# Turning 24 row tiles of a fused two-matmul kernel by DMA instead of on TensorE

## The chip, the cores and the metric

The kernel runs on one core of a Trainium2 chip. The metric is the device time of one execution, in microseconds (us): the time before is the median of three runs. TensorE (PE) multiplies and can also turn (transpose) a 128x128 block; VectorE (DVE) and ScalarE (ACT) do the element-wise work; GpSimd (POOL) and SyncE (SP) issue transfers here. Sixteen DMA engines move the data of the core.

## The reference

The two inputs are `x` (2 batches x 1024 rows x 2048) and a context (2 x 2048 x 2048); a weight of 2048 x 2048 is shared by both batches. Cut to what matters:

```python
# fake_quant: round to integers 0..255 about a zero point of 128, and back
# first product: rows normalised, quantised, times the quantised context of their batch
q1 = fake_quant(layernorm(x), x1_scale, x1_zp)
q2 = fake_quant(ctx_4096, x2_scale, x2_zp)
x = x + tanh(g_xattn) * matmul(q1, q2)
# second product: rows normalised again, quantised to -128..127 by each row's maximum,
# times a weight that is rounded to -1, 0 or 1
n = layernorm(x)
s = 127 / max(abs(n), axis=-1)
q = clip(round(n * s), -128, 127) / s
tw = clip(round(weight / mean(abs(weight))), -1, 1)
x = x + tanh(g_ffn) * einsum('bsi,oi->bso', q, tw) * mean(abs(weight))
```

## The kernel before

**Tiles.** The rows are 16 row tiles of 128 rows: 0 to 7 are batch 1, 8 to 15 batch 2. Eight row tiles of `x` (`resid`) are resident; a tile of batch 2 takes the place of the tile of batch 1 with the same number less 8, once that tile's result is stored. Everything else of size lives in the `arena`, 32 slots of 4 KB in each of 128 partitions (`NS`): loads of context and weight take two neighbouring slots, a quantised context unit takes one, a turned row tile takes one, and the eight quantised weight blocks one each. A second pool, `bytes_`, holds quantised rows as signed bytes (`NB`, 4 buffers of 128x2048, the pool `q8`). In PSUM there are three tiles `mm` of 128x1024 f32 for products and two tiles `tr` for turns.

**Steps.** For each batch: `norm1` takes the mean and variance of a pair of row tiles on DVE (L531, L536), a root on ACT (L540), scale and bias on DVE (L476 to L550), and the cast to bytes on ACT (L567). `first` (L622) multiplies a turned row tile by eight context units for one half of the columns (h is 0 or 1; 32 matmuls in eight steps), and DVE adds the result to `resid` (L628). Context units are loaded (L589), cast on ACT (L593) and clipped on DVE (L597). `norm2` does the second norm for a pair: a square on ACT (L660), its maximum on DVE (L666), a chain of small operations, and the cast to bytes on ACT (L716). The second product uses f16 rows and the ternary weight in fp8. In batch 1 it is `couple` (tiles 0 to 3, L759) and `plain` (tiles 4 to 7, L805); in batch 2 it is `seven` (L930), which computes each pair of row tiles with seven block products in place of eight, from sums of row halves (L895 to L902) and from sums and differences of weight blocks. Those are formed on DVE in `differences` (L842), written to DRAM (L861) and fetched back later (L871). DVE adds the second product to `resid` (L743), and SP stores it (L750). The weight is read twice: first for its mean (L977, L990, L992), then to be quantised (L1028), turned (L1035) and clipped (L1043, L1045).

**Turning a row tile.** `turn_steps` is the function that the change is about. A quantised row tile is 128 rows of 2048 bytes. Seen as 1024 two-byte values it is eight blocks of 128x128, and PE turns each block, a pair of bytes as one value, into a `tr` tile (L494). The pairs are then opened: two copies of 128x1024 bytes each, on ACT or DVE, whichever ends sooner, read the bytes from PSUM with a stride of two and write them as f16 into the tile's arena slot (L502). The byte buffer is free once PE has read it. All 32 turns go this way (16 tiles, two norms), and so do the 16 weight rows.

**The order.** No engine's order is written by hand. Each step is recorded with its engine (or a choice of engines), a weight in us, a due time, the keys that it reads and writes, and the buffers that it takes and gives back. `Order.run` plays the steps against a model: each engine does one step at a time, a transfer occupies one common DMA server for `dma` us and lands `LANDING` (2.0 us) later, and of the steps that could start first the one with the earliest due time is picked. `work_back` goes through the result backwards and gives every step a new due time. `give_out` repeats this 12 times and emits the instructions in the order of the best play, so that the order on every queue, SP's and POOL's among them, is fixed before the kernel runs. An engine works through its own list strictly in that order and waits where an operand is late. Some steps also have a hold, a time in the model before which they don't start: loads of batch 2, and `differences` at 210.

Of the kernel before, what the change touches and what calls it, by code (L numbers as in the profile page):

```python
# [11 lines left out]
I16 = mybir.dt.int16  # L12
F8 = mybir.dt.float8e4
AF = mybir.ActivationFunctionType
ALU = mybir.AluOpType
# [8 lines left out]
class Plan:  # L24
# [9 lines left out]
    def step(self, engine, weight, due, do, rd=(), wr=(), take=None, give=(), dma=0.0, hold=0.0):  # L34
        n = len(self.steps)
        after = set()
        for key in rd:
            if key in self.writer:
                after.add(self.writer[key])
        for key in wr:  # L40
            after.update(self.readers.pop(key, ()))
            if key in self.writer:
                after.add(self.writer[key])
            self.writer[key] = n
        for key in rd:
            self.readers.setdefault(key, []).append(n)
        after.discard(n)
        self.steps.append((engine, weight, due, do, after, take, tuple(give), dma, hold))
        return n
# [58 lines left out]
class Order:  # L108
# [64 lines left out]
    def run(self, due):  # L173
        steps, N = self.steps, len(self.steps)
        waits = [len(s[3]) for s in steps]
        early = [s[7] for s in steps]
        pools = {k: [(0.0, -1)] * n for k, n in self.sizes.items()}
        left = dict(self.users)
        till = {}
        free, open_ = {}, {}  # L180
        dma_free, dma_last = 0.0, -1
        begin, end, where, slots = [0.0] * N, [0.0] * N, [None] * N, [None] * N
        pred = [[] for _ in steps]
        links = self.links = [{} for _ in steps]
        last = {}
        order = []

        def put(n):
            for e, w in steps[n][0]:
                open_.setdefault(e, {})[n] = w  # L190

        for n in range(N):
            if not waits[n]:
                put(n)
        for _ in range(N):
            best = None
            for e, cand in open_.items():
                fe = free.get(e, self.START.get(e, self.BRANCH))
                for n, w in cand.items():
                    at = early[n]  # L200
                    if at < fe:
                        at = fe
                    if best is not None and at > best[0] + 1e-6:
                        continue
                    take = steps[n][4]
                    if take:
                        at = max(at, self.room(pools[take[0]], *take[1:]))
                        if at == float("inf"):
                            continue
                    if len(steps[n][0]) > 1:  # L210
                        key = (at, due[n], n, at + w, e)
                    else:
                        key = (at, due[n], n, 0.0, e)
                    if best is None or at < best[0] - 1e-6 or key[1:] < best[1:]:
                        best = key
            if best is None:
                self.stuck = [n for c in open_.values() for n in c], order, slots
                return None
            at, _, n, _, e = best
            ways, _, _, _, take, give, dma, _ = steps[n]  # L220
            if len(ways) > 1:
                ends = []
                for e2, w2 in ways:
                    ends.append((max(at, free.get(e2, self.BRANCH)) + w2, e2, w2))
                fin, e, w = min(ends)
                at = fin - w
            else:
                w = ways[0][1]
            for e2, _ in ways:
                del open_[e2][n]  # L230
            if take:
                pool = pools[take[0]]
                idx = slots[n] = self.pick(pool, at, *take[1:])
                for i in idx:
                    if pool[i][1] >= 0:
                        pred[n].append(pool[i][1])
                        links[n][pool[i][1]] = True
                    pool[i] = (float("inf"), -1)
            if e in last:
                pred[n].append(last[e])  # L240
            last[e] = n
            begin[n] = at
            where[n] = e
            fin = at + w
            free[e] = fin
            if dma:
                if dma_last >= 0:
                    pred[n].append(~dma_last)
                dma_free = max(dma_free, fin) + abs(dma)
                dma_last = n  # L250
                fin = dma_free + self.LANDING
            end[n] = fin
            order.append(n)
            for m, i in give:
                for j in range(steps[m][4][1]) if i is None else (i,):
                    left[m, j] -= 1
                    t = till.get((m, j))
                    if t is None or fin + self.LAG > t[0]:
                        t = (fin + self.LAG, n)
                    till[m, j] = t  # L260
                    if not left[m, j]:
                        pools[steps[m][4][0]][slots[m][j]] = t
            for m in self.follow[n]:
                same = len(steps[m][0]) == 1 and steps[m][0][0][0] == e and not dma
                t = fin + (0.0 if same else self.LAG)
                if t > early[m]:
                    early[m] = t
                waits[m] -= 1
                if not waits[m]:
                    put(m)  # L270
        return order, begin, end, where, slots, pred
# [72 lines left out]
def centred(  # L344
# [15 lines left out]
    nc = tc.nc  # L360
# [5 lines left out]
    MT, OT = M // P, O // P  # L366
# [1 line left out]
    H, U = 1024, 512  # L368
    NQ = N // U
    I8 = mybir.dt.int8  # L370
    NS, NB = 32, 4
    SLOT = 2048

    const = ctx.enter_context(tc.tile_pool(name="const", bufs=1))
# [28 lines left out]
    def slot16(s):  # L403
        return arena[:, s * SLOT : (s + 1) * SLOT]
# [30 lines left out]

    Q_COST = {"PRE": 0.5, "SP": 0.5, "POOL": 0.7}
    turned = {}

    def parameters():
        s = {}  # L440
# [32 lines left out]
    def rsqrt(v, sd):  # L473
# [7 lines left out]
        nc.vector.scalar_tensor_tensor(r, e, 1.5, r0, ALU.add, ALU.mult)  # L481
        return r

    def turn_steps(t, key, q, q_by, due, name, pieces=1):

        s = {}

        def turn(i, slots=None):
            if slots is not None:
                s["pt"] = tr[slots[0]]  # L490
            pt = s["pt"].bitcast(F16).rearrange("p (c r) -> p c r", c=C)
            v = q["q"].bitcast(F16)
            for c in range(i * C // pieces, (i + 1) * C // pieces):
                nc.tensor.transpose(pt[:, c, :], v[:, ts(c, P)], ident)  # L494

        def spread(h, engine, slots=None):
            if h == 0:
                turned[name, t] = slots[0]
            d = slot16(turned[name, t]).rearrange("p (c j m) -> p c j m", c=C, j=2)
            v = s["pt"].bitcast(I8).rearrange("p (c m j) -> p c j m", c=C, j=2)  # L500
            n = C // 2
            (nc.scalar.copy if engine == "ACT" else nc.vector.tensor_copy)(  # L502
                d[:, ts(h, n)], v[:, ts(h, n)]
            )

        by = None
        for i in range(pieces):
            n = step(
                "PE", 0.05 + 0.55 / pieces, due - 50, (lambda i: lambda slots=None: turn(i, slots))(i),
                rd=[key("q", i)], wr=[key("pt", i)], take=None if i else ("tr", 1),  # L510
                give=[q_by] if i == pieces - 1 else [],
            )
            by = by if i else n
        ways = (("ACT", 1.1), ("DVE", 1.3))
        first_ = step(
            ways, 0, due - 20, lambda e, slots: spread(0, e, slots), rd=[key("pt", 0)], wr=[(name, t, 0)],
            take=("ar", 1, 0, home_t), give=[by],
        )
        step(
            ways, 0, due - 20, lambda e: spread(1, e), rd=[key("pt", pieces - 1), (name, t, 0)],  # L520
            wr=[(name, t, 1)], give=[by],
        )
        turned[name, t, "by"] = first_
# [357 lines left out]
    def seven(ta, tb, due, final=False):  # L881
# [22 lines left out]
        qa, qb = ([("qT", t, i) for i in range(2)] for t in (ta, tb))  # L904
        by = step("DVE", 0.7, due - 3, lambda slots: sums(0, slots), rd=qb, wr=[("S", ta, 1)], take=("ar", 2, 0, pairs_d))
        step("DVE", 0.7, due - 3, lambda: sums(1), rd=qa[:1], wr=qb[:1] + [("S", ta, 3)])
        step("DVE", 0.7, due - 3, lambda: sums(2), rd=qa[:1] + [("S", ta, 1)], wr=[("S", ta, 2)])
        step("DVE", 0.7, due - 3, lambda: sums(3), rd=qa[1:] + [("S", ta, 2)], wr=[("S", ta, 4)])
        products = (
            ("P1", "A", lambda: half(ta, 0), (0, 0), qa[:1], True, (ta, 0)),  # L910
            ("P2", "C", lambda: half(ta, 1), (0, 1), qa[1:], True, (ta, 0)),
# [109 lines left out]
    def weight_turn(ot, due):  # L1021
# [15 lines left out]
        def clip(h, engine, slots=None):  # L1037
# [10 lines left out]
            "ACT", 2.1, due, quant, rd=[("wl", ot), ("sw",)], wr=[key("q")], take=("q8", 1),  # L1048
            give=[wl[ot]["by"]],
        )  # L1050
        p = step("PE", 0.6, due - 50, turn, rd=[key("q")], wr=[key("pt")], take=("tr", 1), give=[by])
        for h in range(2):
            need = [key("pt")] + ([("w", q, 0, h)] if o else [])
# [946 lines left out]
```

## Time and profile before

| What | Value |
|---|---|
| median of three runs | 492.32 us (491.85, 492.32, 495.02) |
| the profiled execution | 494.64 us, its span 492.9 us |
| busy: PE, DVE, ACT, POOL | 457.8, 335.1, 262.8, 21.7 us |
| PE's products: first (L622), second of batch 1 (L759, L805), second of batch 2 (L930) | 229.8; 58.5 and 55.9; 97.5 us |
| PE's turns: rows (L494), weight (L1035) | 256 and 128 instructions |
| copies out of the turns of rows (L502) | 39 on ACT, mean 1.01 us; 25 on DVE, mean 1.22 us |
| moved by DMA | 102.20 MB, mean 207 GB/s |

The span runs from the first to the last instruction of the profiled execution. Busy times are sums over an engine's instructions, without waits. A PE instruction is modelled as longer than its share of PE's time, since matmuls overlap: 1024 of L622 at a mean of 383 ns are busy for 229.8 us together. The granted TensorE clock was at full speed (0.998 in the mean). In time, the first product of batch 1 runs from about 39 to 156 us, the second of batch 1 from 131 to 271 us (the two are mixed between 131 and 156), the first of batch 2 from 271 to 388 us and the second of batch 2 from 388 to 487 us.

### The profile page before, as it was taken

What the parts mean: (1) busy time and instruction counts of PE and PEld (TensorE: products, weight loads), DVE (VectorE), ACT (ScalarE), POOL (GpSimd) and SP (SyncE); (2) the same over time, 40 slices, a digit from 0 to 9 for tenths busy, and PEclk for the clock granted to TensorE, in tenths of its full rate; (3) what the DMA queues carried; (4) which work ended last, traced back from release to release, by engine and by line L of the source; (5) the groups of instructions that cost most, each with busy time, mean ns of one, the idle gap of its engine ahead of it and who ended that gap; (6) DMA issues with size and microseconds to landing.
All of it is one profiled execution on the core that took longest, in us unless ns stands there. A gap on an engine that the chain in (4) does not pass through costs nothing.

```text
span 492.9 us, 6309 instructions
## 1 busy us (share of the span) xinstructions
PE 457.8 (93%) x2564; PEld 225.6 (46%) x2564; DVE 335.1 (68%) x522; ACT 262.8 (53%) x203; POOL 21.7 (4%) x39
## 2 busy tenths in 40 slices
PE   0489999999999898999998989999999999999995
PEld 0134444445576654444444435444444444444442
DVE  4778973588599897769997877223578887343432
ACT  3678987687799988831117678101366853000000
POOL 0000000000002120021011100000000000000000
PEclk9999999999999999999999999999999999999999
DMA  6999988990445985399999750053000012231304
GB/s 208 397 423 421 421 319 332 420 429 41 172 172 231 367 302 211 91 343 391 422 345 325 257 215 1 1 179 163 1 0 1 1 43 88 85 128 44 128 8 169
DMA packets 21853, 102.20 MB, mean 207 GB/s; under 512 B 1976, under 2 KB 1976, under 8 KB 16696
## 3 DMA queue, kind: packets, MB, share of 16 engines
q1 hardware_dynamic: 15008, 67.11, 34.2%
q0 software_dynamic: 6800, 34.61, 19.6%
q8 instruction: 22, 0.36, 0.3%
q14 instruction: 15, 0.12, 0.1%
q10 hardware_dynamic: 8, 0.00, 0.0%
HBM read 80.74 MB, written 20.97 MB: 206 GB/s over the span
## 4 chain that ended last, share of the span: by engine, by line
PE 65%; DMA 14%; issue 12%; DVE 3%; ACT 3%; SPq 1%; POOL 1%; POOLq 0%; ACTq 0%
PE mm L622 41%; PE mm L930 20%; DMA arena<-in_ctx_dram 14%; PE tr L494 2%; ACT arena L593 1%; ACT bytes L567 1%; PE mm L805 1%; SPq L1961 1%; DVE strip L666 1%; POOL arena L589 1%; DVE arena L1045 1%; DVE arena L502 0%; DVE resid L743 0%; PE mm L759 0%; POOL arena L977 0%
## 5 line engine op out<-in xcount | busy, mean ns | idle before, releaser
L622 PE MATMUL mm<-arena 128*128 128x512 f16 x1024 | 229.8, 383 | 7.9 <-DVE arena L597 4.6
L622 PEld LDWEIGHTS <-arena 128*128 128x128 f16 x1024 | 99.6, 99 | 125.0 <-issue 9.3
L743 DVE SCALAR_TENSOR_TENSOR resid<-mm,am,resid 128x1024 f32<-128x1024 f32 (+1 forms) x53 | 58.1, 1097 | 59.7 <-PE mm L930 47.9
L930 PE MATMUL mm<-arena 128*128 128x512 fp8e4 x448 | 97.5, 379 | 0.0
L593 ACT ACTIVATE arena<-arena,scal 128x2048 int16<-128x2048 f32 x32 | 63.3, 1999 | 47.3 <-DMA arena<-in_ctx_dram 36.4
L628 DVE SCALAR_TENSOR_TENSOR resid<-mm,scal,resid 128x1024 f32<-128x1024 f32 x32 | 40.9, 1278 | 49.4 <-PE mm L622 38.1
L930 PEld LDWEIGHTS <-arena 128*128 128x128 f16 x448 | 43.7, 98 | 51.9
L759 PE MATMUL mm<-arena 128*128 128x128 fp8e4 (+1 forms) x448 | 58.5, 288 | 1.7 <-DVE resid L743 1.7
L805 PE MATMUL mm<-arena 128*128 128x512 fp8e4 x256 | 55.9, 379 | 0.0
L660 ACT ACTIVATE arena<-resid,strip 128x2048 f32<-128x2048 f32 x16 | 32.0, 1998 | 39.5 <-DVE strip L654 35.4
L502 ACT CAST arena<-tr 128x1024 f16<-128x1024 int8 x39 | 37.8, 1011 | 16.9 <-PE tr L494 7.5
L759 PEld LDWEIGHTS <-arena 128*128 128x128 f16 x448 | 33.4, 98 | 24.1 <-issue 2.0
L666 DVE TENSOR_REDUCE strip<-arena 128x1 f32<-128x2048 f32 x16 | 36.5, 2280 | 5.1 <-ACT arena L660 5.1
L531 DVE BATCH_NORM_STATS2 stats<-resid 128x6 f32<-128x512 f32 x64 | 39.7, 675 | 0.0
L805 PEld LDWEIGHTS <-arena 128*128 128x128 f16 x256 | 24.9, 98 | 29.5
L567 ACT ACTIVATE bytes<-resid,strip 128x2048 int8<-128x2048 f32 (+1 forms) x17 | 33.0, 1987 | 7.7 <-DVE strip L550 5.9
L716 ACT ACTIVATE bytes<-resid,strip 128x2048 int8<-128x2048 f32 x16 | 32.7, 2087 | 6.7 <-DVE strip L689 6.7
L842 DVE TENSOR_TENSOR arena<-arena 128x2048 fp8e4<-128x2048 fp8e4 x16 | 36.0, 2281 | 0.0
L502 DVE CAST arena<-tr 128x1024 f16<-128x1024 int8 x25 | 30.3, 1218 | 7.1 <-PE tr L494 6.8
L1028 ACT ACTIVATE bytes<-arena,scal 128x2048 int8<-128x2048 f32 x16 | 31.3, 1999 | 0.8 <-DVE scal L1014 0.8
L1045 DVE TENSOR_SCALAR arena<-tr 128x1024 fp8e4<-128x1024 int8 x23 | 27.3, 1216 | 6.1 <-PE tr L1035 6.1
L494 PE MATMUL tr<-ident,bytes 128*128 128x128 f16 x256 | 20.6, 225 | 11.5 <-ACT bytes L567 9.2
(59 smaller groups left out, 184.5 us busy)
## 6 DMA issues: line engine op xcount, KB each, us to landing
arena<-in_ctx_dram SPq DMA_DIRECT2D x16, 1024.0 KB, 15.4
arena<-in_L_ffn_weight_dram SPq DMA_DIRECT2D x16, 1024.0 KB, 12.6
arena<-in_ctx_dram POOLq DMA_DIRECT2D x16, 1024.0 KB, 8.7
out_dram<-resid SPq DMA_DIRECT2D x31, 512.0 KB, 4.7
arena<-in_L_ffn_weight_dram POOLq DMA_DIRECT2D x9, 1024.0 KB, 6.6
resid<-in_x_dram POOLq DMA_DIRECT2D x8, 1024.0 KB, 11.6
resid<-in_x_dram SPq DMA_DIRECT2D x7, 1024.0 KB, 14.7
awayT<-arena SPq DMA_DIRECT2D x8, 512.0 KB, 7.5
```

The source lines that it names most:

```text
L502: (nc.scalar.copy if engine == "ACT" else nc.vector.tensor_copy)(d[:, ts(h, n)], v[:, ts(h, n)])
L531: nc.vector.bn_stats(stats6[:, t % 4, c, :], res(t)[:, ts(c, 512)])
L567: nc.scalar.activation(q["q"][:, ts(g, w)], res(t)[:, ts(g, w)], AF.Identity, bias=s["bi"][:, i : i + 1], scale=s["sc"][:, i : i + 1],)
L593: nc.scalar.activation(slot16(slots[0]).bitcast(I16), s["w"], AF.Identity, scale=rs2)
L622: nc.tensor.matmul(pm[t][:, ts(q, U)], a[:, c, j, :], o[:, j, ts(q, U)], start=(c + j == 0), stop=(c + j == C),)
L628: nc.vector.scalar_tensor_tensor(v, pm[t], g1, v, ALU.mult, ALU.add, accum_out=acc[:, i : i + 1])
L666: nc.vector.tensor_reduce(s["vm"][:, n + i : n + i + 1], s["dev", t], AX.X, ALU.max)
L743: lambda: nc.vector.scalar_tensor_tensor(v, ps(), am2[:, t : t + 1], v, ALU.mult, ALU.add),
L759: nc.tensor.matmul(ps[:, o0 * P : o1 * P], a[:, c, j, :], w[:, j, o0:o1], start=(c + j == 0), stop=(c + j == C),)
L805: nc.tensor.matmul(s["pm"][:, ts(i, U)], a[:, c, j, :], w[:, j, :], start=(c + j == 0), stop=(c + j == C),)
L842: nc.vector.tensor_tensor(slot8(s[k, n])[:, w], slot8(at(a))[:, w], slot8(at(b))[:, w], op, saturate=False)
L930: nc.tensor.matmul(s[bank][:, ts(n, U)], a[:, c, j, :], v[:, c, j], start=new and c + j == 0, stop=c + j == 4, skip_group_check=not new,)
```

## The change

For the row tiles of batch 2 in both norms, and for all tiles of batch 1 in the second norm (`by_dma`, 24 of the 32 turns), a new function `turn_far` takes the place of PE's turn. One DMA on SP's queue turns the row tile's bytes, as 128x1024 two-byte values in eight blocks, from `bytes_` into the upper half of the tile's own arena slot. Two copies then open the pairs within the slot: the first (on ACT or DVE) reads the first half of the bytes and writes the slot's lower half; the second (on ACT only) reads the rest and writes the upper half, where the bytes themselves lie. The slot is taken and the byte buffer held from the issue of the DMA; the buffer is given back when the DMA has landed. The model gets 1.1 us on SP for the issue, 1.4 us on the common DMA server, and a landing 2.8 + 2.0 us after the issue whatever else is queued. There are five byte buffers instead of four. In `seven`, the slot of the pair's first tile is given back only when the two sums that read it (L900, L902) are done as well. The tiles of batch 1 in the first norm and the weight rows are turned as before; the branch for weights in the diff is not taken, since `by_dma` holds no weight.

```diff
-                fin = dma_free + self.LANDING
+                fin = dma_free + self.LANDING if dma > 0 else fin - 2 * dma + self.LANDING
...
-    NS, NB = 32, 4
+    NS, NB = 32, 5
...
+    by_dma = {(k, t) for k, lo in (("aT", MT), ("qT", 0)) for t in range(lo, 2 * MT)}
...
+    def turn_far(t, key, q, q_by, due, name):
+        def turn(slots):
+            turned[name, t] = slots[0]
+            d = slot16(slots[0]).bitcast(I16)[:, H:].rearrange("p (c r) -> p c r", c=C)
+            nc.sync.dma_start_transpose(d, q["q"].bitcast(I16))
+
+        def spread(h, engine):
+            d = slot16(turned[name, t]).rearrange("p (c j m) -> p c j m", c=C, j=2)
+            v = slot16(turned[name, t])[:, H:].bitcast(I8).rearrange("p (c m j) -> p c j m", c=C, j=2)
+            n = C // 2
+            (nc.scalar.copy if engine == "ACT" else nc.vector.tensor_copy)(d[:, ts(h, n)], v[:, ts(h, n)])
+
+        n = turned[name, t, "by"] = step(
+            "SP", 1.1, due, turn, rd=[key("q", 0)], wr=[(name, t, 0), (name, t, 1)], take=("ar", 1, 0, home_t),
+            give=[q_by], dma=-1.4,
+        )
+        step((("ACT", 1.1), ("DVE", 0.75)), 0, due, lambda e: spread(0, e), wr=[(name, t, 0)])
+        step("ACT", 1.1, due, lambda: spread(1, "ACT"), rd=[(name, t, 0)], wr=[(name, t, 1)])
+
     def turn_steps(t, key, q, q_by, due, name, pieces=1):
+        if (name, t) in by_dma:
+            return turn_far(t, key, q, q_by, due, name)
...
-        step("DVE", 0.7, due - 3, lambda: sums(2), rd=qa[:1] + [("S", ta, 1)], wr=[("S", ta, 2)])
-        step("DVE", 0.7, due - 3, lambda: sums(3), rd=qa[1:] + [("S", ta, 2)], wr=[("S", ta, 4)])
+        step("DVE", 0.7, due - 3, lambda: sums(2), rd=qa[:1] + [("S", ta, 1)], wr=[("S", ta, 2)], give=[turned["qT", ta, "by"]])
+        step("DVE", 0.7, due - 3, lambda: sums(3), rd=qa[1:] + [("S", ta, 2)], wr=[("S", ta, 4)], give=[turned["qT", ta, "by"]])
```

## The prediction

> **What bounds the kernel now.** I read the busy shares first, then a table of the engines by stage, then the chain of work that ended last, then the groups of instructions and the landing times of single DMA lines. The page's first part:
>
> ```profile
> PE 457.8 (93%) x2564; PEld 225.6 (46%) x2564; DVE 335.1 (68%) x522; ACT 262.8 (53%) x203; POOL 21.7 (4%) x39
> ```
>
> TensorE is busy for 457.8 of 492.9 us. The 35.1 us that are left lie mostly at the ends: 21.6 us before 40 us, some 6 us after the last product, and about 7.5 us in between. The stages say where those 7.5 are (columns: stage, its length, then busy us and count of PE, PEld, DVE, ACT, POOL, the granted clock, the DMA share and GB/s):
>
> ```profile
> 138.00:165.00 27.00, 24.68 (x331) 19.88 (x329) 26.45 (x39) 27.00 (x20) 4.57 (x8) 1.00 0.65 255
> 165.00:202.00 37.00, 35.08 (x228) 18.46 (x226) 31.09 (x42) 32.67 (x23) 3.74 (x5) 1.00 0.75 267
> ...
> 264.00:288.00 24.00, 21.05 (x121) 10.43 (x122) 20.79 (x36) 14.93 (x12) 1.24 (x2) 1.00 0.85 300
> 288.00:310.00 22.00, 22.00 (x127) 10.92 (x127) 15.90 (x37) 20.49 (x18) 0.56 (x1) 1.00 0.14 49
> 310.00:388.00 78.00, 78.00 (x387) 36.34 (x386) 41.60 (x82) 28.28 (x27) 0.00 (x0) 1.00 0.15 55
> ```
>
> The reader should see two kinds of stage. After 288 us PE has no gap, ACT and DVE have room and the DMA engines are nearly idle: whatever leaves PE there shortens the kernel one for one. From 138 to 202 us ACT and DVE are as full as PE (ACT 27.00 of 27), and from 264 to 288 us, where batch 2 begins, PE already waits 3 us. There a shorter PE helps only if its operands come no later. The chain in order of time (start, length, what) shows the second place:
>
> ```profile
> 264.94 0.62 PE tr L494 x8
> 265.56 5.18 PE mm L805 x24
> 270.74 0.45 PE tr L494 x8
> 271.19 10.36 PE mm L622 x48
> ...
> 285.91 0.92 issue
> 286.83 1.02 ACT arena L502
> ```
>
> Tile 8's bytes are done at 264.90 us, its turn ends at 265.56, and PE covers the copies with 24 products of the last tile of batch 1. After the 64 products of tiles 8 and 9 with the first half of the context, PE stands 2 us at 285.9 for the copy of tile 10. That copy itself waited for something that came at about 286.8, although its turn had ended at 282; a write to DRAM of a weight difference issued at 278.5 that holds an arena slot fits (such writes take 7.5 us, below).
>
> **The change part by part.** Removed, on PE: eight transposes (L494) for each of 24 row tiles (batch 1's second norm, batch 2's first and second norm, eight each). In the chain each such turn takes 0.45 us ("270.74 0.45 PE tr L494 x8"), so 24 x 0.45 = 10.8 us, 3.6 for each of the three groups. Removed too: 48 of the 64 copies of L502, counted in the timeline as 34 on ACT and 14 on DVE. Their price, and the nearest rows for the copies that replace them:
>
> ```profile
> L502 ACT CAST arena<-tr 128x1024 f16<-128x1024 int8 x39 | 37.8, 1011 | 16.9 <-PE tr L494 7.5 <-PE mm L622 6.4 <-DVE arena L502 3.0
> L502 DVE CAST arena<-tr 128x1024 f16<-128x1024 int8 x25 | 30.3, 1218 | 7.1 <-PE tr L494 6.8
> L597 DVE TENSOR_SCALAR arena<-arena 128x2048 f16<-128x2048 int16 x32 | 21.2, 684 | 5.1 <-ACT arena L593 5.1
> L567 ACT ACTIVATE bytes<-resid,strip 128x1024 int8<-128x1024 f32 x2 | 2.4, 1234 | 1.3 <-DVE strip L550 1.3
> ```
>
> Added: 48 copies of 128x1024 bytes to f16 from SBUF. The second half of each tile may only run on ACT: 24 there, between 1.0 us (the PSUM row) and 1.23 (the SBUF row of the same length); I take 1.1. The first half may go to DVE; the trace has no such copy, so its price lies between 0.34 (half of L597's 684 ns) and 1.22 (L502 on DVE); I take 0.75, nearer to L597, which reads SBUF as this copy does. Where ACT is full, tiles 2 to 7, it was 4 copies on ACT and 8 on DVE, 4 x 1.01 + 8 x 1.22 = 13.8 us, and becomes 6 x 1.1 + 6 x 0.75 = 11.1 us. As ACT and DVE also share the weight copies (L1043, L1045), I put this at nothing; if all halves went to ACT it would be 12 x 1.1 - 4 x 1.01 = 9.2 us more on a full ACT, which is why I keep it in the upper bound. A fifth byte buffer and the later release in the product of seven cost no instruction.
>
> Added, on the SP queue: 24 turns, one DMA of 256 KB each. Issue: a plain DMA takes SP 0.33 us (L750); the order assumes 1.1, and SP is free for that, since no weight load is issued after 100 us and the first store is at 175.8. Behind a turn on SP stand stores and the writes of weight differences; POOL's loads of x wait for stores (14.4 us over two waits), so SP's delay can reach POOL. From issue to landing the trace has no turn. The nearest rows are these, writes of 512 KB under nearly full DMA engines, and stores of 256 and 512 KB:
>
> ```profile
> L861 SPq DMA_DIRECT2D awayT<-arena x8: 319/326/327, 216.2 to 278.5; - x8
> ...
> DMA to landing us min/median/max: 5.1/7.5/8.1
> ```
>
> ```profile
> L750 SPq DMA_DIRECT2D out_dram<-resid x33: 332/332/348, 175.8 to 487.6; - x33
> ...
> DMA to landing us min/median/max: 2.6/4.4/11.2
> ```
>
> So 2.6 to 11.2 us. The order of the changed kernel is planned on 1.1 + 2.8 + 2.0 = 5.9 us (its own weights, not a measurement). I take 6.5: between the median store (4.4) and the median write of twice the bytes (7.5), a little above the plan.
>
> The Trainium skill speaks against this edit ("VectorE: DVE Perf Modes", sections "The three transpose paths" and "Rules for kernel authors"): a 128x128 block takes 390 ns on TensorE and 1309 ns by DMA, and TensorE is to be used where PSUM will do as destination. Eight such blocks in a row would be an estimated 10.5 us of landing, against 3.1 us on TensorE; the trace shows 0.45 us for eight in the stream of products, so the page's TensorE figure does not hold here. "Advanced Engine Details and Errata", section "X-Bar Transpose (TRN2)", says instead that such DMAs are about as fast as plain ones, which would leave my 6.5 or less. By the first page the sum below would end near my slower rival, by the second near my faster one.
>
> Now the path, place by place. (1) Second norm of batch 1, gain 3.6. Tiles 0 and 1 have their bytes by 117.3 us and are used at 130.6: 13 us of cover. Tiles 2 to 7 (three pairs, cast to bytes from 139.7 to 187.1) fall where ACT is full. There the copy on ACT stands in its queue where the plan expects the landing; each 0.1 us of later landing stops ACT for 0.1 us, and the weight casts (L1028) and squares (L660) behind it, and then PE, which waits for weights. Three pairs x (6.5 - 5.9) = 1.8 us lost. (2) First norm of batch 2, gain 3.6. Tile 8: 264.9 + 6.5 + 1.0 = 272.4 instead of 271.2, while PE runs out of batch 1 up to 4 us sooner: between 1.2 and 5.2 lost, less the 1.24 us that PE today waits for the bytes before its transposes; I take 2. Tile 10: with its slot free at 286.8 as now, 286.8 + 6.5 + 1.0 = 294.3 against 287.9, 6.4 lost if PE has nothing else. It has: 15 of the 16 context units are cast (L593) by 273 us, so the products of tiles 8 and 9 with the second half, 2 x 7 x 0.864 = 12.1 us, can be put first, if DVE has clipped those units (L597, 0.68 us each, DVE 87% busy). I take 2 of the 6.4. Tiles 12 to 15 have over 6 us of products ahead of them. (3) Second norm of batch 2, gain 3.6, lost nothing: tile 8's bytes are there at 359 us and first used at 388, the last pair's at 404.5 with sevens of 24 us each still ahead. Without that cover it would be the landing again, 6.5 us once.
>
> Sum: 10.8 - 1.8 - 2 - 2 = 5.0 us less. The profiled execution took 494.64 us (span 492.9 and 1.7 around it), so 489.6 on its terms; the median of the runs is 492.32, 2.3 below that one, and so 487.3.
>
> **The rivals.** A, all of it is gained: the order is made anew, puts the second-half products into the gap at 286 us and starts the norm of tile 8 sooner. For it: DVE loses its slowest copies, and PSUM's two turn buffers serve weights alone. Against it: arena slots are short there, and a turn now holds its slot and its bytes until the landing. 492.3 - 10.8 = 481.5; with today's waits of 2.0 and 1.24 us gone too, 478.3.
>
> B, slower: late landings stop ACT. One mechanism, at five places: the pairs 2/3, 4/5, 6/7, 8/9 and 10/11, where DMA shares of 0.65 to 0.87 mean that a turn shares the engines with loads. At the 9.6 us that POOL's context loads need in the median, 5 x (9.6 - 6.5) = 15.5 us on top of the forecast: 502.8. It decides from the point where the landings pass 6.5 + 5.0 / 5 = 7.5 us: above that the kernel is slower than before. For it: the writes' median is just 7.5 us at twice the bytes. Against it: half the bytes, and DMA engines with room before 165 us (a share of 0.65).
>
> C, no change: before 288 us PE isn't the bound; slots, x loads and ACT set the time at which batch 2 begins, and the PE time saved comes back as waits. Then only what leaves PE after 288 us counts, 8 x 0.45 + 4 x 0.45 = 5.4, less up to 6.4 for tile 10: 486.9 to 493.3, say 491. For it: the chain runs through context loads from 151 to 265 us. Against it: PE is 61.71 of 62 us busy from 202 to 264.
>
> D, the turns aren't done as planned (many small packets, a turn much longer than its bytes): that is B with a longer landing: at twice mine, 13 us, 487.3 + 5 x 6.5 = 519.8.
>
> **How the numbers follow.** Forecast (483 to 492): 0.45. A: 0.17. C: 0.13. B: 0.20. D: 0.05. The likeliest gives 487.3. A measurement of this kernel tells about 1% (4.9 us) from no change: below 487.4 is faster, above 497.2 slower. Faster: all of A, half of the forecast (0.23) and a little of C: 0.42. Slower: B and D but for their cheap end, and a tail of the forecast: 0.27. Within: 0.31. The range reaches down into A (480.5) and up to B's price (503), which leaves out D and the lower end of A, with about 0.15 in all.
>
> **What would show it.** Right: L494 with 64 instructions in place of 256, L502 with 16, PE busy near 447 us; 24 DMAs on SP from the byte buffers with landings of 5 to 8 us; PE idle between 264 and 295 us of some 5 to 7 us; no gap after 310 us, and the last store some 5 us sooner. Wrong: ACT's copy of turned bytes waiting for DMA in 138 to 202 us by more than 3 us in total (B), landings above 7.5 us, or a PE that stands after 310 us; and a gap at 286 us that is gone speaks for A.

## The result and the profile after

The changed kernel takes 505.38 us in the median of four runs (504.62 to 507.27) against 492.14 us (491.85 to 495.02) for the kernel before: a ratio of 1.0254, 95% interval 1.0213 to 1.0294. It is slower. Here and below a ratio compares with executions of the kernel before from the same session (their medians were 492.1 to 494.2 us) and leaves out executions in a slower state of the chip, which were two of the six of the version without tiles 4 to 7. The profiled execution took 504.62 us, its span is 502.8 us. The page's first part and its clock row:

```profile
PE 451.1 (90%) x2372; PEld 215.7 (43%) x2372; DVE 332.5 (66%) x528; ACT 259.5 (52%) x198; POOL 21.2 (4%) x39
...
PEclk9989999999999599899999889999999999999998
```

PE has 192 instructions fewer and is busy for 6.7 us less than before, but it now stands for 51.7 us of the span (502.8 - 451.1) instead of 35.1. So 16.6 us of new waits, less 6.7, make the 9.9 us by which the span grew. The digit 5 in the clock row is new as well. The stages that were shown of the kernel before (same columns: stage, its length, PE, PEld, DVE, ACT, POOL, granted clock, DMA share, GB/s):

```profile
138.00:165.00 27.00, 23.48 (x316) 18.94 (x313) 24.56 (x38) 21.79 (x15) 4.57 (x8) 1.00 0.85 275
165.00:202.00 37.00, 28.32 (x160) 14.04 (x161) 21.16 (x30) 28.87 (x20) 2.80 (x4) 0.86 0.72 219
...
264.00:288.00 24.00, 17.58 (x82) 7.74 (x81) 14.82 (x31) 10.85 (x8) 2.64 (x4) 0.94 0.99 327
288.00:310.00 22.00, 22.00 (x94) 9.63 (x93) 19.62 (x35) 15.82 (x12) 1.11 (x2) 0.91 0.90 257
310.00:388.00 78.00, 78.00 (x363) 35.35 (x362) 41.48 (x86) 27.56 (x25) 0.00 (x0) 1.00 0.23 72
```

After 288 us PE has no gap, as before. From 138 to 202 us not only PE but also ACT, which was busy for 27.00 of 27 and 32.67 of 37 us there, now stands: it is busy for 21.79 and 28.87 us. The chain of work that ended last names what they stood for (start, length, what). The lines named here that stand behind `turn_far` have numbers that are 24 higher than in the kernel before (the first product is L646, the weight casts are L1052); in `turn_far`, L491 issues a turn and L497 is its two copies:

```profile
154.39 17.76 DMA arena<-bytes
172.15 0.02 issue
172.17 1.05 ACT arena L497
173.22 0.05 issue
173.27 3.19 PE mm L829 x8
...
194.62 8.21 DMA arena<-bytes
...
274.81 12.00 DMA arena<-bytes
286.81 0.02 issue
286.83 0.70 DVE arena L497
287.54 0.05 issue
287.58 112.83 PE mm L646 x512
```

`DMA arena<-bytes` is a turn. Three turns are on the chain, 17.76, 8.21 and 12.00 us from issue to landing, and each is followed by the copy that opens its pairs (L497) and, at once or after a few steps of DVE, by a PE that starts again. The waits of the stage from 138 to 206 us (engine and line, what it waited for, us in total, times, longest) agree:

```profile
POOL arena L613 <- ACT bytes L1052: 32.7, 3, 23.4
...
DVE arena L1069 <- ACT bytes L1052: 12.3, 1, 12.3
ACT arena L497 <- DMA arena<-bytes: 12.0, 1, 12.0
PEld L829 <- ACT arena L497: 12.0, 1, 12.0
PE mm L829 <- ACT arena L497: 11.8, 1, 11.8
```

ACT stood 12.0 us at the copy. The weight casts (L1052) that follow it in ACT's list, DVE's weight copies (L1069) behind those, and POOL's loads that wait for the casts all stood with it. PE's three large gaps are 11.8 us at 161, 4.8 us at 202 and 6.4 us at 281 us, 23.0 us in all; between 40 us and its last product PE had stood some 7.5 us in the kernel before.

The landing of a turn depends on the time of its issue. First the turns issued from 100 to 206 us, then those from 370 to 435 us (the same line, two stretches):

```profile
L491 SPq DMA_TRANSPOSE arena<-bytes x8: 1232/1723/8515, 114.1 to 200.4; - x8
...
DMA to landing us min/median/max: 4.3/5.5/17.8
```

```profile
L491 SPq DMA_TRANSPOSE arena<-bytes x8: 1231/1234/1557, 374.1 to 432.5; - x8
...
DMA to landing us min/median/max: 2.7/2.8/2.8
```

With DMA engines that are mostly idle a turn lands after 2.7 us. The one issued at 154.4 us stood amid eight loads of 1 MB that POOL issued between 146.9 and 157 us, and took 17.8. The next one kept SP itself busy for 8.5 us instead of 1.23.

### The profile page after: what moved, and what is told of

Same layout as the page of the kernel before. It is cut to its first block, busy times and chain, and to the rows that moved or that the text cites. A ratio compares the mean times of both kernels' runs of the same rounds, so it can differ in the third digit from the quotient of the medians.

```text
span 502.8 us, 6000 instructions
## 1 busy us (share of the span) xinstructions
PE 451.1 (90%) x2372; PEld 215.7 (43%) x2372; DVE 332.5 (66%) x528; ACT 259.5 (52%) x198; POOL 21.2 (4%) x39
## 2 busy tenths in 40 slices
DMA packets 47195, 108.46 MB, mean 216 GB/s; under 512 B 27320, under 2 KB 27320, under 8 KB 42040
## 4 chain that ended last, share of the span: by engine, by line
PE 66%; DMA 19%; DVE 4%; ACT 4%; issue 4%; POOL 0%; SPq 0%; POOLq 0%; ACTq 0%
PE mm L646 39%; PE mm L954 19%; DMA arena<-bytes 8%; DMA resid<-in_x_dram 6%; PE mm L783 6%; DMA arena<-in_ctx_dram 5%; DVE arena L1069 1%; ACT bytes L1052 1%; ACT bytes L591 1%; ACT bytes L740 1%; ACT arena L617 1%; DVE resid L767 1%; PE mm L829 1%; ACT arena L497 1%; DMA out_dram<-resid 1%
## 5 line engine op out<-in xcount | busy, mean ns | idle before, releaser
L646 PE MATMUL mm<-arena 128*128 128x512 f16 x1024 | 229.6, 385 | 13.3 <-DVE arena L497 6.4
L646 PEld LDWEIGHTS <-arena 128*128 128x128 f16 x1024 | 100.7, 99 | 135.7 <-issue 13.4
L954 PE MATMUL mm<-arena 128*128 128x512 fp8e4 x448 | 96.9, 379 | 0.0
L829 PE MATMUL mm<-arena 128*128 128x512 fp8e4 x256 | 57.4, 385 | 11.8 <-ACT arena L497 11.8
L783 PE MATMUL mm<-arena 128*128 128x128 fp8e4 (+1 forms) x448 | 59.8, 292 | 4.8 <-DVE resid L767 4.8
L497 ACT CAST arena<-arena 128x1024 f16<-128x1024 int8 x33 | 33.8, 1039 | 34.7 <-DMA arena<-bytes 16.1
L1069 DVE TENSOR_SCALAR arena<-tr 128x1024 fp8e4<-128x1024 int8 x29 | 34.5, 1217 | 16.3 <-ACT bytes L1052 12.3
L1052 ACT ACTIVATE bytes<-arena,scal 128x2048 int8<-128x2048 f32 x16 | 31.4, 1989 | 0.0
L1016 ACT ACTIVATE junk<-arena 128x2048 int8<-128x2048 f32 x12 | 22.9, 1905 | 4.3 <-DMA arena<-in_L_ffn_weight_dram 4.2
L621 DVE TENSOR_SCALAR arena<-arena 128x2048 f16<-128x2048 int16 x32 | 21.1, 690 | 4.4 <-ACT arena L617 4.4
```

The lines of the kernel that those rows point to most:

```text
L646: nc.tensor.matmul(pm[t][:, ts(q, U)], a[:, c, j, :], o[:, j, ts(q, U)], start=(c + j == 0), stop=(c + j == C),)
L783: nc.tensor.matmul(ps[:, o0 * P : o1 * P], a[:, c, j, :], w[:, j, o0:o1], start=(c + j == 0), stop=(c + j == C),)
L829: nc.tensor.matmul(s["pm"][:, ts(i, U)], a[:, c, j, :], w[:, j, :], start=(c + j == 0), stop=(c + j == C),)
L954: nc.tensor.matmul(s[bank][:, ts(n, U)], a[:, c, j, :], v[:, c, j], start=new and c + j == 0, stop=c + j == 4, skip_group_check=not new,)
L1069: nc.vector.tensor_scalar(d, v, -1.0, 1.0, ALU.max, ALU.min, saturate=False)
```

## The experiments

The theory: turns that meet a queue of loads land late, ACT and DVE stand in their fixed order behind the copy that waits for it, and PE runs dry. Against it stood the copies and holds of the new path, the order made anew, and the start of batch 2 as a loss of its own.

**Parts of the change alone.** Each of the first three keeps only some of the turns on DMA; the rest is as in the changed kernel.

```diff
-    by_dma = {(k, t) for k, lo in (("aT", MT), ("qT", 0)) for t in range(lo, 2 * MT)}
+    by_dma = {("qT", t) for t in range(MT, 2 * MT)}   # second norm of batch 2
+    by_dma = {("aT", t) for t in range(MT, 2 * MT)}   # first norm of batch 2
+    by_dma = {("qT", t) for t in range(MT)}           # second norm of batch 1
+    by_dma = set()                                    # none
```

> Only the second norm of batch 2 (8 of the 24 turns) goes by DMA. Theory (late landings): what costs time is that a turn whose packets alternate with those of queued loads lands 8 to 18 us after its issue, and that ACT and then PE stand behind the copy that waits for it. These eight turns meet no loads, so they land after 2.7 to 2.8 us as in the changed kernel, and PE loses 8 x 0.45 us of turns: 492.1 - 3.6 = 488.5 us, no gap in PE after 310 us. Rival (engine work): the copies from the slot and the longer hold of slots and byte buffers cost the time wherever they are: 492 us or more.

Measured: ratio 0.9939 (0.9905 to 0.9973), some 3.0 us less (median 491.86 against 494.17 us). The eight turns landed after 2.7 to 3.3 us and PE had no gap after 310 us. The theory's 3.6 us lie inside the interval; engine work alone doesn't cost the time.

> Only the first norm of batch 2 goes by DMA. Theory (late landings): the turn of tile 8 lands some 12 us after its issue beside the loads, PE stands about 6 us before the first product of batch 2, and the 3.6 us of turns are gained: 492.1 + 6.4 - 3.6, or 494 to 497 us. Rival (the two late pairs of batch 1 alone cost it all): the start of batch 2 is only late because batch 1 was, and this kernel takes 488 to 490 us.

Measured: ratio 0.9923 (0.989 to 0.9956), some 3.8 us less. This is a miss for the theory's number, and the median of 490.03 us lies at the edge of the rival's range: turns of the first norm are a gain by themselves. They did land late, but in this order they were issued earlier. Two of its turns, from 240 to 250 us:

```profile
L491 SPq DMA_TRANSPOSE arena<-bytes x2: 2588/3738/4887, 245.2 to 247.9; - x2
...
DMA to landing us min/median/max: 11.0/11.0/11.0
```

A landing of 11 us, and PE had no idle time from 165 to 310 us: the first product of batch 2 came at 265.0 us, 20 us after the first issue. In the changed kernel the first of these turns was issued only at 274.8 us, 6.4 us before PE ran out of work. The 3.8 us are not the turns alone, since the whole order was made anew: against the kernel before, PE stands 3.5 us less from 138 to 202 us and 4.5 us more from 310 to 388 us.

> Only the second norm of batch 1 goes by DMA. Theory (late landings): the turns of tiles 4 to 7 meet the loads of the weight and of batch 2's context, land after 8 to 18 us, PE stands 12 and 5 us for them and its clock falls for a while: 500 to 505 us. Rival (bandwidth or order at the start of batch 2 is what counts): 489 to 493 us.

Measured: 507.17 us, ratio 1.0252 (1.0204 to 1.03), as much as the loss of the whole change. One turn, issued at 152.5 us, landed after 18.4 us; PE stood 14.1 us in one piece at 158 us:

```profile
PE mm L783 <- DVE resid L767: 18.6, 2, 14.1
```

Here it was DVE that stood behind the late copy, and PE's results behind DVE. The three parts do not add up to the whole: 2.5 - 0.6 - 0.8 makes a loss of 1.1%, and all 24 turns together lose 2.5%. Each version has an order of its own, and in that of the changed kernel the turns of batch 2 cost the 6.4 us at 281 us.

> No turn goes by DMA; the fifth byte buffer, the later release of a slot in the product of seven and the order made anew stay. Both theories: 492 us within 1.5. If the new order or the buffer itself is to blame for part of the loss, the time differs by more than 2 us.

Measured: ratio 0.9985 (0.9955 to 1.0015). The fifth buffer, the later release and the making of a fresh order are not the cause by themselves.

**The loads taken away.** The same order of all steps, but POOL's loads of weight and context carry a sixteenth of their bytes, once in the kernel before and once in the changed kernel.

```diff
-            queue(name).dma_start(out=s["w"].rearrange("p (j n) -> p j n", j=2), in_=src)
+            d = s["w"].rearrange("p (j n) -> p j n", j=2)
+            n = 64 if b else H
+            queue(name).dma_start(out=d[:, :, 0:n], in_=src[:, :, 0:n])
...
-            queue(name).dma_start(out=s["w"], in_=weight[ts(ot, P), :])
+            n = 128 if name == "POOL" else I
+            queue(name).dma_start(out=s["w"][:, 0:n], in_=weight[ts(ot, P), 0:n])
```

> The kernel before, with POOL's loads of the weight and of batch 2's context cut to a sixteenth of their bytes (128 of 2048 columns, 64 of 1024); the rest of those slots keeps older data. All steps and their order are as before. It is the base for the next run. Both theories: 487 to 492 us, since PE waits for few loads.

> The changed kernel with the same cut of POOL's loads, so that the turns meet hardly any load; all steps and their order are those of the changed kernel. Theory (late landings): the turns land after 2.7 to 6 us, PE's gaps of 12, 5 and 6 us go and the clock stays up: 7 to 11 us faster than the kernel before with small loads, 478 to 484 us. Rival (engine work, slots, the new order): it stays slower than the kernel before with small loads, about 500 us.

Measured: 491.09 us (490.4 to 491.85) for the kernel before and 479.51 us (478.12 to 480.7) for the changed kernel, both with small loads: the change now gains 11.6 us where it cost 13. Against the full kernel before, the ratios are 0.9948 (0.9922 to 0.9973) and 0.9726 (0.9668 to 0.9784). The changed kernel's page and its turns with small loads:

```profile
PE 446.9 (94%) x2372; PEld 214.9 (45%) x2372; DVE 331.6 (70%) x528; ACT 259.2 (54%) x198; POOL 21.5 (5%) x39
...
PEclk9999999999999999999999999999999999999999
```

```profile
L491 SPq DMA_TRANSPOSE arena<-bytes x24: 1231/1237/2494, 113.7 to 406.0; - x24
...
DMA to landing us min/median/max: 2.7/3.0/5.8
```

All 24 turns land within 5.8 us. PE is busy for 446.9 us, 10.9 less than in the kernel before (457.8) and 10.4 less than in that kernel with small loads (457.3); the turns had been put at 10.8. In the changed kernel with its full loads PE was busy for 451.1: the 4.2 us between fit the lower clock after the gaps (granted in the mean 0.974, against 0.999 here). The instructions, their order, copies and holds are the same; what differs is the bytes that POOL's loads move. The same cut gains the kernel before only 0.5%, so it is not that smaller loads make any order faster.

**The plan told of a later landing.** The kernel's work stays as in the changed kernel; only the model that makes the order changes.

```diff
-                fin = dma_free + self.LANDING if dma > 0 else fin - 2 * dma + self.LANDING
+                fin = dma_free + self.LANDING if dma > 0 else fin + (12.0 if dma == -1.41 else 2.8) + self.LANDING
...
-            give=[q_by], dma=-1.4,
+            give=[q_by], dma=-1.41 if (name, t) in late else -1.4,
```

> The changed kernel, but the model that makes the order is told a landing 12.0 + 2.0 us after the issue for the turns of tiles 4 to 7 in the second norm and tiles 8 to 11 in the first norm of batch 2 (2.8 + 2.0 for the rest). Theory (the loss is that ACT and DVE stand in their queues behind a copy whose bytes are late, and not the lateness itself): the copies come later in their lists, the weight casts go first, PE's gap near 160 us shrinks to under 4 us: 488 to 495 us. Rival (PE has nothing else to do until those tiles are turned): 500 us or more.

Measured with these 8 turns in `late`: 496.1 us, ratio 1.0072 (1.0033 to 1.0111). More than half of the loss is gone, but both expectations missed: PE still stood 9.6 us at 159 us. This time DVE stood 7.7 us behind a copy of a turn that was not in `late` (tile 2 or 3, issued at 151.7 us, landed after 14.8 us), and ACT 6.9 us behind DVE.

> The changed kernel with all 16 turns of the second norm of batch 1 and the first norm of batch 2 planned with a landing 12.0 + 2.0 us after the issue. In the run where only 12 of them were, PE still stood 9.6 us behind a copy of tile 2 or 3 that DVE waited for. Theory (standing behind a late copy is the loss): this gap goes too, 486 to 491 us. Rival (PE has no other work there): 494 us or more.

Measured with these 16 turns in `late`, where the run before had 8 and not 12: 488.68 us, within the theory's range,, ratio 0.9917 (0.9886 to 0.9948). The same 24 turns by DMA now make the kernel faster than before. In the new order they also meet fewer loads (landing 3.8 us in the median, 10.4 at most), so this run doesn't separate standing behind a late copy from being late; with the run of the small loads it shows that the loss is in how landings and order fit, not in the work.

**A version that is faster than both.**

```diff
-    by_dma = {(k, t) for k, lo in (("aT", MT), ("qT", 0)) for t in range(lo, 2 * MT)}
+    by_dma = {(k, t) for k in ("aT", "qT") for t in range(MT, 2 * MT)}               # batch 2 only
+    by_dma = {...the 24...} - {("qT", t) for t in range(4, MT)}                      # all but tiles 4 to 7
```

> The 16 turns of batch 2 go by DMA (both norms), those of batch 1 do not. Theory (the loss sits in the second norm of batch 1, where late landings stop ACT, DVE and PE; the rest gains): the gains of the two parts add up, 0.6% and 0.8% below the kernel before, so a ratio of 0.986, some 6.8 us. Rival (the late start of batch 2 in the changed kernel was a loss of its own): a ratio of 0.995 or more.

Measured: 486.11 us (485.56 to 487.54), ratio 0.9858 (0.9813 to 0.9903), a gain of 1.4% as the sum of its two parts has it. PE is busy for 452.4 us of a span of 485.7. The first of its turns are issued at 246.8 us, 19 us before the first product of batch 2, and land after 11 us; PE has no idle time from 165 to 310 us.

> As the changed kernel, but the second norm of tiles 4 to 7 is turned on PE: 20 turns by DMA. Theory (only turns that meet a queue of loads cost time, and tiles 0 to 3 meet few: they landed after 3.2 to 5.5 us): 4 x 0.45 = 1.8 us better than with batch 2 alone, a ratio of 0.982 to 0.986. Rival (any turn in the stage where ACT is full costs time): slower than batch 2 alone.

Measured: ratio 0.9875 (0.9801 to 0.9948). The 1.8 us that four more turns should bring are not seen, and whether they cost anything can't be told: the intervals overlap. PE stands 2.5 us between 138 and 202 us, against 0.75 with the turns of batch 2 only, so what leaves PE there seems to come back as waits.

**One turn beside loads.** Nothing of the computation is left in these two; they time single transfers. The first:

```python
gate(); wide(8); later()                               # 8 loads of 1 MB on POOL, then some 6 us
nc.sync.dma_start_transpose(turned, src.bitcast(I16))  # the turn on SP
```

> Nothing of the computation is left: one turn of 128x1024 two-byte values from issue to landing, A alone, C to G each beside loads of 1 MB that POOL issued some 6 us earlier: C eight with pieces of 8 KB, D eight of 4 KB, E eight of 2 KB, F eight of 1 KB, G four of 8 KB; B is a plain copy of the same 256 KB alone, H the same beside eight loads of 8 KB pieces. Theory (each of the turn's some 66 small packets per DMA engine waits for one packet of the loads): A 2.7 us; C and D 10 to 20 us, until the loads are through; E and F less, by the size of the packets; G shorter than C, as the loads end sooner; H under 6 us, since a plain copy has an eighth of the packets. Rival (the engines are shared by bytes): C to G all about 3 to 5 us, like H.

Measured: alone, a turn 3.1 us and a plain copy 2.3 us. Loads of the next situation began before the turn of the one before had landed, so C to G can't be told apart by their loads; beside such steady traffic a turn took 9.1 to 21.2 us and a plain copy 7.6.

> As the measurement of one turn beside loads, but every situation starts only when all transfers of the one before have landed, and the turn is issued some 3 us after the first load. A alone; B eight loads of 1 MB with pieces of 8 KB, C of 4 KB, D of 1 KB; E four and F two loads of 8 KB pieces; G a plain copy of 256 KB beside eight loads; then eight loads alone. Theory 1 (a turn's many small packets each wait for one packet of the loads, so it lands when the loads are nearly through, whatever the size of the pieces): B, C and D 14 to 20 us, E 6 to 10, F 4 to 6, G under 8. Theory 2 (it waits for one piece of the loads): D under half of B. Theory 3 (shared by bytes): B to F all 3 to 5 us.

Measured, from issue to landing: A 3.1; B 21.4; C 17.3; D 18.3; E 11.4; F 6.8; the plain copy G 8.1. B's turn and its eight loads of 8 KB pieces:

```profile
L50 SPq DMA_TRANSPOSE dst<-src x1: 1357/1357/1357, 27.9 to 27.9; - x1
...
DMA to landing us min/median/max: 21.4/21.4/21.4
```

```profile
L34 POOL DMA_DIRECT2D load<-in_L_ffn_weight_dram x8: 528/528/662, 25.7 to 29.4; - x8
...
DMA to landing us min/median/max: 5.3/12.4/19.7
```

The turn landed at 49.3 us, about with the last of the loads (29.4 + 19.7 = 49.1), although by the times of issue some three of the eight were issued after it. Eight such loads with nothing beside them landed after 18.7 us at most, against 19.7 here: it is the turn that waits, the loads hardly do. E and F land within 1 us of their last load as well (118.9 and 118.2, 128.4 and 127.4); C and D land at 69.3 and 96.9 us, 7 and 8 us ahead of it; there only some four and three of the eight loads were issued before the turn. Smaller pieces shorten the landing little (C, D), so theory 2 falls, and the shares by bytes of theory 3 fall with B. Theory 1 fits the order of the landings, though B, E, F and G each lie up to 1.4 us above its ranges. That it is packets taking turns was not shown: what speaks for it is that a turn has some 1056 packets for its 256 KB ((47195 - 21853) / 24, from the packet counts of the profiles after and before) and that a plain copy of the same bytes lands in 8.1 us.

## Why the prediction was wrong

**What bounds the kernel: right.** PE's 10.8 us were there to be gained: with small loads PE is busy for 446.9 us, near the 447 that the prediction named.

**Copies: right.** L497 takes 683 ns on DVE (0.75 taken) and 1044 ns on ACT (1.1 taken). On the chain they take 3.5 us in all, each time behind a turn.

**The landing: this step failed.** The prediction took one value, 6.5 us, for all 24 turns, from the median store and the median write of weight differences. As a middle value it was good, for the median of the 24 landings is 5.3 us; but the time went by the longest ones. The landing depends on the loads around the turn: 2.7 to 2.8 us where the DMA engines are mostly idle, 4.3 to 5.5 for those issued from 114 to 140 us, and 17.8, 8.2 and 12.0 us for the three turns on the chain. The rows that the prediction used were of plain transfers; beside eight loads a plain copy lands in 8.1 us where a turn needs 17 to 21, so the 11.2 us of its upper bound was too low as well.

**Place 1, second norm of batch 1: the term that was mis-sized.** 1.8 us were put down for three pairs, as 6.5 - 5.9 each. The single turn of 154.4 us landed 12 us after the plan's 5.9 and stopped ACT for 12.0 and PE for 11.8; PE's gap of 4.8 us follows the landing of 8.2, for which DVE stood 2.1 us, and some steps of DVE. The loss has the form that was described there, ACT behind a late copy and the weight casts behind ACT; its size was wrong. That the lower clock after a gap adds to it (some 4.2 us in all) was in no step.

**Place 2, first norm of batch 2: right in its form, too small.** 4 us of loss were put down, 2 of them for tile 8 at a landing of 6.5 us. In the changed kernel tile 8's turn took 12.0 us, PE had 6.4 us of work left when it was issued (274.8 to 281.2), and PE stood 6.4 us. Not all of this was handed on from batch 1: with small loads, in the same order and with batch 1 hardly held up, the turn is issued only 8.6 us ahead of the first product of batch 2 (254.6 and 263.2), less than a landing of 12. Where the order issues these turns 19 to 20 us ahead, as in the versions with batch 2 only and with its first norm only, they land after 11 us and PE does not stand for them.

**Place 3, second norm of batch 2: right.** Landings of 2.7 to 2.8 us, no gap. From the first product of batch 2 to the last product the changed kernel needs 209.5 us (287.58 to 497.12), 6.3 less than before (271.03 to 486.83); 7.2 us of turns had left that stretch or its start.

**The rivals.** B, at 0.20, was the case: late landings stop ACT and the kernel loses. Its price of 502.8 us assumed 9.6 us at five places; what came was one landing of 17.8 and two of 8 and 12, and a lower clock, so that 505.4 lies near this price is partly luck. Something of D is in it as well: beside eight loads a turn takes far longer than a plain copy of its bytes (17.3 to 21.4 against 8.1 us), but not where the DMA engines are mostly idle. A's full gain came only with small loads (479.5 us). C's time was missed, but its claim that nothing before 288 us can be gained is not refuted by the version with batch 2 only: its gain of 7.0 us (4.8 to 9.2) includes the 5.4 that C allows. With small loads the claim fails, for the change then gains 11.6. Of the signs that the prediction named for being wrong two were there, ACT's wait for DMA in 138 to 202 us (12.0 us, over 3) and landings above 7.5 us; PE did not stand after 310 us.

**The pages.** The Trainium skill's page "VectorE: DVE Perf Modes", section "The three transpose paths", gives 1309 ns for one block by DMA; eight in a row would be an estimated 10.5 us. Alone the turn of eight took 2.7 to 3.1 us, so the measurement decides against this estimate. The Trainium skill's page "Advanced Engine Details and Errata", section "X-Bar Transpose (TRN2)", has such DMAs as fast as plain ones; alone that roughly holds (3.1 against 2.3 us), beside eight loads it doesn't (17.3 to 21.4 against 8.1).

## What to carry to other kernels

A transfer that replaces engine work has to be priced at the place where it is issued, with the loads that are queued there, and not by a median over the kernel: here turns of the same size took from 2.7 to 17.8 us. On engines that work in a fixed order, the price of a late transfer includes all that stands behind the first instruction that waits for it: here one landing stopped ACT, DVE and PE for some 12 us each. Plan such an instruction late (that this alone helps was not shown, since the later plan also met fewer loads), or move only those transfers whose stage has idle DMA engines or cover of the length of the load queue. Moving 16 of the 24 turns gave 1.4% where moving all 24 cost 2.5%.

## What was not expected of the hardware

A turn by DMA of 256 KB waits for most or all of the loads that were queued around it (17.3 to 21.4 us beside eight loads of 1 MB, for pieces of 1 to 8 KB), while a plain copy of the same bytes doesn't (8.1 us, one measurement). SP was held for up to 8.5 us by the issue of one turn in the stage of loads, against 1.23 us without. In PE's gap of 11.8 us the granted clock fell to half and was still there when PE began again at 173.3 us (columns as in the table of stages), so that the gap cost more than its length: the first eight products took 3.19 us, where sixteen of the same line take 3.62 us at 191 us.

```profile
172.00:176.00 4.00, 2.73 (x7) 1.04 (x8) 0.00 (x0) 3.80 (x3) 0.00 (x0) 0.51 0.08 17
```
